# Second layer of a two-layer network: another order of one period's calls, other slots for four of them

## The chip, the cores and the metric

The kernel runs on one core of a Trainium2 chip. The core has five engines that work side by side, each through its own queue in order: PE (TensorE, matrix products), ACT (ScalarE, functions of single elements), DVE (VectorE) and POOL (GpSimd) for arithmetic on tiles, SP (SyncE), which here only starts transfers. They wait for one another through semaphores. The metric is the device time of one execution in microseconds, the median of several runs.

## The reference

Input is x, 8 images of 128 channels and 128 x 128 points, float32. The first layer (a dilated convolution, Fourier transforms, channel attention and a gate) takes about the first 2,000 us and is not changed. The second layer, on its result x:

```python
y = conv2d(x, conv_w, padding=1) + conv_b              # 3x3, 128 -> 128 channels
seq = y.reshape(B * H * W, 8, 16)                      # 8 tokens of 16 channels
xz = einsum('nld,ed->nle', seq, in_proj_w); xi, z = split(xz)
xc = silu(causal_depthwise_conv(xi) + conv1d_b)        # 32 channels, 4 taps
dt, Bm, Cm = split(xc @ x_proj_w.T, [1, 17])
dt = softplus(dt * dt_proj_w + dt_proj_b)
h = exp(dt * A) * h + dt * Bm * xc                     # 16 states per channel, over the 8 tokens
ym = (sum(h * Cm, states) + D * xc) * silu(z)
out = ym @ out_proj_w.T
xp = silu(group_norm(out.reshape(B, C, H, W), 4 groups))
return x + xp
```

## The kernel before

The second layer works in blocks of four image rows (512 points in the free dimension), 256 blocks in all. The partitions hold channels for the convolution, then channel and token for the projections, then 8 channels x 16 states for the recurrence, with one token and 16 channels (two such halves, 1,024 elements) as the unit of work. Such a unit is called by a number s from 0 to 15: token s // 2, half s % 2. What happens to one unit:

- `spread_a(i, s, slot)` and `spread_u(i, s, slot)` (L840, PE) multiply dt by A, or spread the input u, onto 128 partitions, into one of three PSUM tiles s0, s1, s2, the slots. Each uses two groups of 32 rows of PE's array: those of even s are the lower ones, those of odd s the upper ones.
- `exps(i, s)` (L851, ACT) takes the exponential in place in the slot.
- `inject(i, s)` (L864, DVE; L862, POOL for s = 4 and 5) makes the new tile h = spread u times B.
- `decay(i, s)` (L875, DVE) multiplies the exponential in its slot by h of unit s - 2; for s = 12 and 13 (L873) it writes a new h, for 14 and 15 (L870) it multiplies into a product with C.
- `add(i, s)` (L880, DVE), for s = 2 to 11, adds the slot to h, and the slot is free.
- `weigh(i, s)` (L886, POOL) makes hc = h times C, and `collect(i, t)` (L987, PE) sums the states of token t into PSUM tile yps. `cross` (L892, DVE), `end_products` (L935, POOL), `ends_sum` (L952 and L957, PE), `own_terms` (L964, DVE) and `own_add` (L971, PE) do the same for the last tokens without an h of their own.

Around these stand, per block, the nine taps of the convolution (`conv`, L734, PE), `biased` (L741, ACT, the bias, out of PSUM tile pm), `turn` (L747, PE, four transposes of that result into pm), `turned` (L752, ACT), the projections (`project_x`, `project_z`, `project_dt`, `project_bc`, `project_out`, PE) with the functions behind them (`silu_x`, `silu_z`, `softplus`, `states`, ACT), `inputs` (L792, POOL, u = dt times xc), `skip` (L980, ACT, D times xc into yps), `gated` (L994, DVE), `result` and `spread_of` (ACT, sums for the norm), and `last_load`, `last_act`, `last_sum`, `last_store`, which finish an image that has its norm. Once in 32 blocks `norm` runs the group norm's statistics through DVE, PE and ACT.

SP starts the transfers: `lay_states` copies rows of B and C (tiles all_b and all_c) over 128 partitions into bb0, bb1, cc0, cc1; `lay_first`, `lay_own`, `lay_own_first`, `lay_ends`, `lay_cross` and `store_inputs` with `lay_inputs` move the pieces for the last tokens and for POOL's injects.

The order is written out by hand. The tuple ORDER (from L1093) lists 154 calls as (function, ahead, arguments), and the loop behind it runs the whole tuple for i from -4 to 258, each call on block i + ahead. One pass is called a period. Five engines are set to keep that order (no scheduler moves anything), so the tuple gives each engine's queue, and a call that waits holds up all calls behind it on its engine. Semaphores follow from the tiles: a spread waits until its slot's last reader is done, a new h or hc until the readers of the tile nine allocations before are done (pools of 9), turn, the projections and `ends_sum` until tile pm is free.

Of the kernel before, what the change touches and what calls it, by code (L numbers as in the profile page):

```python
# [595 lines left out]
def layer1(ctx, tc, x1, w1, c1, out):  # L596
# [489 lines left out]
    def last_store(i):  # L1086
# [4 lines left out]

    FIRST = (lay_ends, lay_first, lay_own, lay_own_first, end_products, ends_sum, own_terms)
    ORDER = (  # L1093
        (load, 4), (store_inputs, 0, 2), (last_store, -2), (exps, -1, 10), (lay_first, -1), (end_products, -1),
        (exps, -1, 13), (lay_own, -1), (add, -1, 11), (conv, 2, 0, 0), (project_z, 1, 0), (silu_z, 1),
        (decay, -1, 10), (decay, -1, 13), (conv, 2, 1, 0), (add, -1, 10), (weigh, -1, 8), (spread_u, 0, 2, 2),
        (spread_a, -1, 15, 1), (gated, -1, 0), (inject, 0, 2), (spread_a, -1, 12, 0), (conv, 2, 2, 0),
        (exps, -1, 15), (lay_cross, -1), (weigh, -1, 15), (lay_inputs, 0, 2), (weigh, -1, 13), (weigh, -1, 10),
        (project_x, 1, 2, 0), (exps, -1, 12), (lay_states, 0, 1, 0), (silu_x, 1), (decay, -1, 15),
        (decay, -1, 12), (cross, -1, 15), (conv, 2, 3, 0), (spread_u, 0, 1, 0), (spread_a, 0, 2, 1),  # L1100
        (spread_u, 0, 7, 2), (exps, 0, 2), (inject, 0, 1), (conv, 2, 4, 0), (skip, -1, 1), (spread_u, 0, 3, 0),
        (inputs, 0, 1), (inject, 0, 7), (spread_a, -1, 14, 2), (exps, -1, 14), (conv, 2, 5, 0),
        (collect, -1, 4), (decay, 0, 2), (inject, 0, 3), (conv, 2, 6, 0), (weigh, -1, 14), (add, 0, 2),
        (spread_a, 0, 3, 0), (lay_states, 0, 0, 1), (spread_u, 0, 8, 1), (cross, -1, 14), (conv, 2, 7, 0),
        (last_act, -1), (lay_ends, 0), (weigh, -1, 11), (decay, -1, 14), (collect, -1, 5), (inject, 0, 8),
        (weigh, -1, 12), (exps, 0, 3), (decay, 0, 3), (conv, 2, 8, 0), (keep, -2), (spread_u, 0, 9, 1),
        (spread_a, 0, 4, 2), (lay_own_first, -1), (add, 0, 3), (biased, 2), (inject, 0, 4), (norm, -3),
        (turn, 2), (exps, 0, 4), (inject, 0, 9), (decay, 0, 4), (last_load, 0), (turned, 2),
        (spread_a, 0, 6, 0), (exps, 0, 6), (spread_of, -2), (ends_sum, -1), (weigh, 0, 2), (spread_a, 0, 5, 1),
        (add, 0, 4), (own_terms, -1), (exps, 0, 5), (inject, 0, 5), (decay, 0, 6), (spread_u, 0, 6, 2),  # L1110
        (project_dt, 1, 0, 0), (inject, 0, 6), (decay, 0, 5), (collect, -1, 7), (spread_a, 0, 7, 2),
        (collect, -1, 6), (softplus, 1, 0), (exps, 0, 7), (project_bc, 1, 0), (weigh, 0, 3), (own_add, -1, 1),
        (lay_states, 0, 1, 1), (inputs, 1, 0), (states, 1, 0), (add, 0, 6), (last_sum, -1), (weigh, 0, 4),
        (add, 0, 5), (decay, 0, 7), (gated, -1, 1), (spread_u, 0, 11, 1), (spread_a, 0, 8, 0), (skip, 0, 0),
        (add, 0, 7), (project_bc, 1, 1), (weigh, 0, 5), (exps, 0, 8), (inject, 0, 11), (collect, 0, 1),
        (decay, 0, 8), (spread_u, 0, 10, 2), (lay_states, 1, 0, 0), (states, 1, 1), (weigh, 0, 7),
        (spread_a, 0, 9, 1), (inject, 0, 10), (add, 0, 8), (project_dt, 1, 1, 0), (own_add, 0, 0),
        (exps, 0, 9), (decay, 0, 9), (collect, 0, 2), (spread_a, 0, 11, 0), (softplus, 1, 1), (add, 0, 9),
        (spread_u, 1, 0, 2), (project_out, -1, 0), (inject, 1, 0), (weigh, 0, 6), (project_out, -1, 1),
        (exps, 0, 11), (result, -1), (spread_a, 0, 10, 1), (decay, 0, 11), (spread_a, 0, 13, 2), (weigh, 0, 9),  # L1120
        (collect, 0, 3),
    )

    TR = 2 * RB
# [42 lines left out]
def network(tc, x, w0, w1, c0, c1, out):  # L1167
    B = x.shape[0]
    with tc.tile_pool(name="dram", bufs=1, space=DRAM) as dram:
        x1 = [dram.tile([C, H, W], F32, name=f"x1_{b}") for b in range(B)]  # L1170
        layer0(tc, x, w0, c0, x1)
        layer1(tc, x1, w1, c1, out)
# [73 lines left out]
```

## Time and profile before

| | |
|---|---|
| Median of 3 runs | 13,595.54 us (13,595.24 to 13,596.91) |
| Profiled execution, its span | 13,597.71 us, 13,594.9 us |
| PE busy | 13,227.2 us (97%) |
| DVE busy | 11,943.4 us (88%) |
| POOL busy | 11,940.1 us (88%) |
| ACT busy | 10,091.1 us (74%), of it table loads for exponentials 1,599.9 us |
| DMA queue of SP | 60.0% of 16 engines |

The first 2,000 us are the first layer; the second fills the rest, and drains in the last 200 us or so. PE's matrix instructions overlap and their ends are modelled, so PE's busy share overstates how full it is. A line of the timeline gives start, duration, engine, source line and operation, output and inputs, shapes, count, and in brackets the idle time before with what ended it. A line of the waits gives total us, times and the longest.

### The profile page before, as it was taken

How to read it: one execution, taken by the hardware profiler on the slowest of the kernel's cores; microseconds unless marked ns; L12 is line 12 of the kernel's file. 1: busy time of each engine (PE TensorE's matmuls, PEld its weight loads, DVE VectorE, ACT ScalarE, POOL GpSimd, SP SyncE). 2: the span in 40 equal slices, each digit the busy share in tenths (PEclk: the TensorE clock that was granted, in tenths of full speed). 3: DMA queues.
4: the chain of work that ended last, by engine and by line, in shares of the span. 5: the costliest groups of instructions: out<-in, count | busy, mean ns of one | idle time of the engine just before them, and what ended most of it. 6: DMA issues, size and time to landing. Idle time of an engine off the chain costs nothing. (4 is left out here: it accounts for less than half of the span.)

```text
span 13594.9 us, 255193 instructions
## 1 busy us (share of the span) xinstructions
PE 13227.2 (97%) x97850; PEld 4812.6 (35%) x97850; DVE 11943.4 (88%) x11710; ACT 10091.1 (74%) x11827; POOL 11940.1 (88%) x6533
## 2 busy tenths in 40 slices
PE   9999999999999999999999999999999999999996
PEld 5676663333333333332333333332333333323332
DVE  3343349999999999999999999999999999999997
ACT  3454367777788878887888878887888788878886
POOL 6766659999899999999999989999999999989996
PEclk9999999999999999999999999999999999999998
DMA  4544455555566666666666666666666666666666
GB/s 132 160 133 125 144 128 135 134 129 135 137 154 149 152 145 153 152 150 147 150 154 150 149 146 151 153 149 148 148 154 152 144 153 150 154 142 154 150 150 177
DMA packets 1183640, 1996.65 MB, mean 147 GB/s; under 512 B 149616, under 2 KB 411824, under 8 KB 1174224
## 3 DMA queue, kind: packets, MB, share of 16 engines
q1 hardware_dynamic: 1181840, 1977.82, 60.0%
q8 instruction: 769, 12.60, 0.4%
q14 instruction: 455, 3.73, 0.1%
q10 hardware_dynamic: 576, 2.50, 0.1%
HBM read 687.75 MB, written 218.10 MB: 67 GB/s over the span
## 5 line engine op out<-in xcount | busy, mean ns | idle before, releaser
L886 POOL TENSOR_TENSOR hc<-h,cc 128x1024 f32<-128x1024 f32 x3584 | 8424.7, 2375 | 308.2 <-PE s L840 219.9
L851 ACT ACTIVATE s<-s 128x1024 f32<-128x1024 f32 x3584 | 3558.2, 1005 | 1185.5 <-PE s L840 1166.7
L840 PE MATMUL s<-dt,m_a 32*128 32x512 f32 x14336 | 3525.2, 638 | 17.0 <-DVE h L880 14.5
L875 DVE TENSOR_TENSOR s<-s,h 128x1024 f32<-128x1024 f32 x2560 | 3134.3, 1224 | 46.0 <-ACT s L851 22.4
L864 DVE TENSOR_TENSOR h<-s,bb 128x1024 f32<-128x1024 f32 x2560 | 3100.6, 1215 | 55.2 <-DMA bb<-all_b 20.2
L880 DVE TENSOR_TENSOR h<-s,h 128x1024 f32<-128x1024 f32 x2560 | 3094.7, 1217 | 54.5 <-DVE s L875 1.8
L840 PE MATMUL s<-u,l_ct 32*128 32x512 f32 x10240 | 2892.2, 641 | 50.2 <-DVE h L873 18.4
L734 PE MATMUL pm<-xin,l_wt 128*32 128x508 f32 (+3 forms) x18432 | 2409.2, 595 | 6.2 <-DVE wk L650 5.5
L987 PE MATMUL yps<-hc,l_ct 128*32 128x512 f32 x14336 | 1889.6, 598 | 61.5 <-ACT yps L980 55.9
L851 ACT ACT_TABLE_LOAD x1247 | 1599.9, 1283 | 235.8 <-DVE h L880 136.6
L840 PEld LDWEIGHTS s<-dt,m_a 32*128 32x128 f32 x14336 | 969.1, 183 | 1275.0 <-DVE h L880 629.7
L840 PEld LDWEIGHTS s<-u,l_ct 32*128 32x128 f32 x10240 | 768.2, 183 | 1438.5 <-DVE h L880 521.2
L862 POOL TENSOR_TENSOR h<-ud,bb 128x1024 f32<-128x1024 f32 x512 | 1220.8, 2384 | 2.4 <-DMA ud<-uw 2.4
L792 POOL TENSOR_TENSOR u<-dt,xc 128x512 f32<-128x512 f32 x512 | 656.0, 1281 | 458.5 <-ACT dt L787 456.6
L734 PEld LDWEIGHTS pm<-xin,l_wt 128*32 128x32 f32 x18432 | 469.3, 109 | 1588.4 <-issue 1586.7
L987 PEld LDWEIGHTS yps<-hc,l_ct 128*32 128x32 f32 x14336 | 394.9, 109 | 1288.8 <-issue 1024.3
L870 DVE TENSOR_TENSOR hc<-s,hc 128x1024 f32<-128x1024 f32 x512 | 623.6, 1218 | 199.4 <-ACT s L851 191.0
L787 ACT ACT_TABLE_LOAD x511 | 655.6, 1283 | 40.9 <-PE pm L782 23.9
L980 ACT ACTIVATE yps<-xc,l_wt 128x512 f32<-128x512 f32 x511 | 352.1, 689 | 403.3 <-DVE ym L994 403.3
L873 DVE TENSOR_TENSOR h<-s,h 128x1024 f32<-128x1024 f32 x512 | 621.5, 1214 | 0.0
L892 DVE TENSOR_TENSOR hc<-s,cbx 128x1024 f32<-128x1024 f32 x512 | 620.4, 1212 | 0.0
L782 PE MATMUL pm<-xc,m_dt 128*32 128x512 f32 x4096 | 545.6, 605 | 1.4 <-ACT yT L752 0.7
(202 smaller groups left out, 15362.6 us busy)
## 6 DMA issues: line engine op xcount, KB each, us to landing
cc<-all_c SPq DMA_DIRECT2D x1792, 256.0 KB, 5.5
bb<-all_b SPq DMA_DIRECT2D x1536, 256.0 KB, 5.7
ud<-uw SPq DMA_DIRECT2D x1024, 256.0 KB, 4.1
xin<-x SPq DMA_DIRECT2D x152, 768.0 KB, 5.1
xin<-x SPq DMA_DIRECT2D x112, 640.0 KB, 6.6
us<-u SPq DMA_DIRECT2D x1025, 64.0 KB, 1.9
cbx<-cb SPq DMA_DIRECT2D x512, 128.0 KB, 2.4
gn<-xr SPq DMA_DIRECT2D x256, 256.0 KB, 2.2
```

The source lines that it names most:

```text
L734: nc.tensor.matmul(d["pm"][c, a:b, wa:wb], convw[:, t, c], xin[:, r + dy + a - lo:r + dy + b - lo, wa + dx:wb + dx], start=(k == 0), stop= ...
L787: nc.scalar.activation(d["dt", hf], flat(d["pm"]), AF.Softplus, bias=wf("dt_b"))
L792: nc.gpsimd.tensor_mul(d["u", hf], d["dt", hf], d["xc"][:, hf, :])
L840: nc.tensor.matmul(d[name, s][:, q], m[a:a + DI, t % LP, :], d[src, t // LP][a:a + DI, :], start=True, stop=True)
L851: nc.scalar.activation(da, da, AF.Exp)
L862: nc.gpsimd.tensor_mul(h, d["ud", t][:, k:k + GP, :], state_row(i, "bb", t))
L864: nc.vector.tensor_mul(h, d["ups", s], state_row(i, "bb", t))
L870: nc.vector.tensor_mul(d["hc", s], da, d["hc", s])
L875: nc.vector.tensor_mul(da, da, d["h", s - GP])
L880: nc.vector.tensor_add(h, d["da", s], h)
L886: nc.gpsimd.tensor_mul(hc, d["h", s if t < L - 1 else s - GP], state_row(i, "cc", t))
L987: nc.tensor.matmul(d["yps"][g * DI:(g + 1) * DI], gather[:, t % LP, :], d["hc", GP * t + g // GP][:, g % GP], start=False, stop=t in LAST, ...
```

## The change

ORDER holds the same 154 calls in another order. The first and last call of the tuple are others: what stood in the last third or so of a pass now stands at the front of the next, with its block number lowered by one, so that the same work is done. Apart from that turn of the cycle, many calls stand elsewhere among their neighbours, on all engines. Four spreads have other slots: `spread_u` 6 and `spread_a` 4 go to slot 1, `spread_u` 9 and `spread_a` 5 to slot 2. No call is added or removed, and nothing outside the tuple changes.

```diff
@@ -1091,34 +1091,34 @@

     FIRST = (lay_ends, lay_first, lay_own, lay_own_first, end_products, ends_sum, own_terms)
     ORDER = (
-        (load, 4), (store_inputs, 0, 2), (last_store, -2), (exps, -1, 10), (lay_first, -1), (end_products, -1),
-        (exps, -1, 13), (lay_own, -1), (add, -1, 11), (conv, 2, 0, 0), (project_z, 1, 0), (silu_z, 1),
-        (decay, -1, 10), (decay, -1, 13), (conv, 2, 1, 0), (add, -1, 10), (weigh, -1, 8), (spread_u, 0, 2, 2),
-        (spread_a, -1, 15, 1), (gated, -1, 0), (inject, 0, 2), (spread_a, -1, 12, 0), (conv, 2, 2, 0),
-        (exps, -1, 15), (lay_cross, -1), (weigh, -1, 15), (lay_inputs, 0, 2), (weigh, -1, 13), (weigh, -1, 10),
-        (project_x, 1, 2, 0), (exps, -1, 12), (lay_states, 0, 1, 0), (silu_x, 1), (decay, -1, 15),
-        (decay, -1, 12), (cross, -1, 15), (conv, 2, 3, 0), (spread_u, 0, 1, 0), (spread_a, 0, 2, 1),
-        (spread_u, 0, 7, 2), (exps, 0, 2), (inject, 0, 1), (conv, 2, 4, 0), (skip, -1, 1), (spread_u, 0, 3, 0),
-        (inputs, 0, 1), (inject, 0, 7), (spread_a, -1, 14, 2), (exps, -1, 14), (conv, 2, 5, 0),
-        (collect, -1, 4), (decay, 0, 2), (inject, 0, 3), (conv, 2, 6, 0), (weigh, -1, 14), (add, 0, 2),
-        (spread_a, 0, 3, 0), (lay_states, 0, 0, 1), (spread_u, 0, 8, 1), (cross, -1, 14), (conv, 2, 7, 0),
-        (last_act, -1), (lay_ends, 0), (weigh, -1, 11), (decay, -1, 14), (collect, -1, 5), (inject, 0, 8),
-        (weigh, -1, 12), (exps, 0, 3), (decay, 0, 3), (conv, 2, 8, 0), (keep, -2), (spread_u, 0, 9, 1),
-        (spread_a, 0, 4, 2), (lay_own_first, -1), (add, 0, 3), (biased, 2), (inject, 0, 4), (norm, -3),
-        (turn, 2), (exps, 0, 4), (inject, 0, 9), (decay, 0, 4), (last_load, 0), (turned, 2),
-        (spread_a, 0, 6, 0), (exps, 0, 6), (spread_of, -2), (ends_sum, -1), (weigh, 0, 2), (spread_a, 0, 5, 1),
-        (add, 0, 4), (own_terms, -1), (exps, 0, 5), (inject, 0, 5), (decay, 0, 6), (spread_u, 0, 6, 2),
-        (project_dt, 1, 0, 0), (inject, 0, 6), (decay, 0, 5), (collect, -1, 7), (spread_a, 0, 7, 2),
-        (collect, -1, 6), (softplus, 1, 0), (exps, 0, 7), (project_bc, 1, 0), (weigh, 0, 3), (own_add, -1, 1),
-        (lay_states, 0, 1, 1), (inputs, 1, 0), (states, 1, 0), (add, 0, 6), (last_sum, -1), (weigh, 0, 4),
-        (add, 0, 5), (decay, 0, 7), (gated, -1, 1), (spread_u, 0, 11, 1), (spread_a, 0, 8, 0), (skip, 0, 0),
-        (add, 0, 7), (project_bc, 1, 1), (weigh, 0, 5), (exps, 0, 8), (inject, 0, 11), (collect, 0, 1),
-        (decay, 0, 8), (spread_u, 0, 10, 2), (lay_states, 1, 0, 0), (states, 1, 1), (weigh, 0, 7),
-        (spread_a, 0, 9, 1), (inject, 0, 10), (add, 0, 8), (project_dt, 1, 1, 0), (own_add, 0, 0),
-        (exps, 0, 9), (decay, 0, 9), (collect, 0, 2), (spread_a, 0, 11, 0), (softplus, 1, 1), (add, 0, 9),
-        (spread_u, 1, 0, 2), (project_out, -1, 0), (inject, 1, 0), (weigh, 0, 6), (project_out, -1, 1),
-        (exps, 0, 11), (result, -1), (spread_a, 0, 10, 1), (decay, 0, 11), (spread_a, 0, 13, 2), (weigh, 0, 9),
-        (collect, 0, 3),
+        (load, 4), (add, -1, 7), (lay_states, -1, 1, 1), (gated, -2, 1), (decay, -1, 8), (states, 0, 1),
+        (lay_states, 0, 0, 0), (project_dt, 0, 1, 0), (skip, -1, 0), (lay_first, -1), (lay_own, -1),
+        (spread_u, -1, 10, 2), (inject, -1, 10), (spread_a, -1, 9, 1), (exps, -1, 9), (store_inputs, 0, 2),
+        (add, -1, 8), (decay, -1, 9), (collect, -1, 1), (weigh, -1, 6), (own_add, -1, 0), (collect, -1, 2),
+        (spread_u, 0, 0, 2), (weigh, -1, 7), (softplus, 0, 1), (spread_a, -1, 11, 0), (end_products, -1),
+        (lay_cross, -1), (project_out, -2, 0), (add, -1, 9), (inject, 0, 0), (project_out, -2, 1),
+        (spread_a, -1, 10, 1), (spread_a, -1, 13, 2), (lay_states, 0, 1, 0), (exps, -1, 11), (result, -2),
+        (decay, -1, 11), (exps, -1, 10), (conv, 2, 0, 0), (add, -1, 11), (exps, -1, 13), (decay, -1, 10),
+        (decay, -1, 13), (collect, -1, 3), (add, -1, 10), (project_z, 1, 0), (conv, 2, 1, 0),
+        (spread_u, 0, 2, 2), (weigh, -1, 8), (last_sum, -2), (silu_z, 1), (spread_a, -1, 15, 1),
+        (spread_a, -1, 12, 0), (gated, -1, 0), (weigh, -1, 9), (conv, 2, 2, 0), (inject, 0, 2),
+        (weigh, -1, 15), (project_x, 1, 2, 0), (exps, -1, 15), (exps, -1, 12), (cross, -1, 15),
+        (conv, 2, 3, 0), (decay, -1, 12), (spread_u, 0, 1, 0), (decay, -1, 15), (inject, 0, 1), (silu_x, 1),
+        (weigh, -1, 11), (spread_a, 0, 2, 1), (spread_u, 0, 7, 2), (conv, 2, 4, 0), (exps, 0, 2),
+        (inject, 0, 7), (spread_u, 0, 3, 0), (skip, -1, 1), (spread_a, -1, 14, 2), (lay_states, 0, 0, 1),
+        (weigh, -1, 10), (conv, 2, 5, 0), (decay, 0, 2), (weigh, -1, 14), (lay_own_first, -1), (exps, -1, 14),
+        (inject, 0, 3), (inputs, 0, 1), (add, 0, 2), (conv, 2, 6, 0), (last_act, -1), (conv, 2, 7, 0),
+        (spread_u, 0, 6, 1), (lay_inputs, 0, 2), (spread_a, 0, 3, 0), (weigh, -1, 13), (conv, 2, 8, 0),
+        (decay, -1, 14), (collect, -1, 4), (cross, -1, 14), (exps, 0, 3), (inject, 0, 6), (inject, 0, 4),
+        (decay, 0, 3), (last_store, -2), (biased, 2), (norm, -3), (turn, 2), (weigh, -1, 12),
+        (spread_a, 0, 4, 1), (spread_u, 0, 9, 2), (spread_of, -2), (turned, 2), (add, 0, 3), (inject, 0, 9),
+        (ends_sum, -1), (spread_a, 0, 5, 2), (spread_a, 0, 6, 0), (exps, 0, 4), (last_load, 0), (decay, 0, 4),
+        (own_terms, -1), (inject, 0, 5), (weigh, 0, 2), (exps, 0, 5), (project_dt, 1, 0, 0), (exps, 0, 6),
+        (collect, -1, 7), (add, 0, 4), (own_add, -1, 1), (spread_u, 0, 8, 1), (decay, 0, 5), (softplus, 1, 0),
+        (lay_ends, 0), (weigh, 0, 3), (add, 0, 5), (decay, 0, 6), (spread_a, 0, 7, 2), (project_bc, 1, 0),
+        (inject, 0, 8), (collect, -1, 5), (add, 0, 6), (inputs, 1, 0), (exps, 0, 7), (decay, 0, 7),
+        (weigh, 0, 4), (spread_u, 0, 11, 1), (states, 1, 0), (spread_a, 0, 8, 0), (weigh, 0, 5),
+        (project_bc, 1, 1), (keep, -2), (inject, 0, 11), (exps, 0, 8), (collect, -1, 6),
     )

     TR = 2 * RB
```

## The prediction

> **What bounds the kernel now.** Read first: the busy table by stretches, for a stretch in the middle of the second layer.
>
> ```profile
> core 0: us, PE busy (x) PEld busy (x) DVE busy (x) ACT busy (x) POOL busy (x), PEclk, DMA share, GB/s
> 6000.00:7000.00 1000.00, 983.28 (x7466) 306.18 (x7460) 969.31 (x881) 805.36 (x890) 927.95 (x444) 0.99 0.63 150
> ```
>
> PE, DVE and POOL are all above 92%, so busy shares don't name the bound. Read next: the timeline of DVE. One period (one block of four image rows) takes 44.49 us: the median over 105 periods without a group norm, each 44.5. With the entry, the drain and the first layer around them: 256 x 44.49 = 11,389 us, seven periods with a norm add 12.9 us each (a pair with a norm takes 101.9, 2 x 44.49 = 89.0), and 2,115 us lie outside; together the span, 13,594.9. The profiled execution was 13,597.71 us, the median of the timed runs 13,595.54, so I apply the difference to the median.
>
> ```profile
> 6033.17 1.21 DVE L880 TENSOR_TENSOR h<-s,h 128x1024 f32<-128x1024 f32 x1
> 6034.30 0.68 DVE L994 TENSOR_TENSOR ym<-yps,zs 128x512 f32<-128x512 f32 x1
> 6034.90 1.21 DVE L864 TENSOR_TENSOR h<-s,bb 128x1024 f32<-128x1024 f32 x1
> 6036.86 1.23 DVE L870 TENSOR_TENSOR hc<-s,hc 128x1024 f32<-128x1024 f32 x1 [0.75 <-ACT s L851]
> ...
> 6053.17 1.22 DVE L875 TENSOR_TENSOR s<-s,h 128x1024 f32<-128x1024 f32 x1
> 6054.49 1.23 DVE L880 TENSOR_TENSOR h<-s,h 128x1024 f32<-128x1024 f32 x1
> 6055.64 0.68 DVE L964 TENSOR_TENSOR own<-pm,us 128x512 f32<-128x512 f32 x1
> 6056.23 1.22 DVE L875 TENSOR_TENSOR s<-s,h 128x1024 f32<-128x1024 f32 x1
> 6057.36 1.21 DVE L864 TENSOR_TENSOR h<-s,bb 128x1024 f32<-128x1024 f32 x1
> ```
>
> Starts of independent neighbours are 1.13 apart (6056.23 to 6057.36), a short one (own, gated) takes 0.60. A decay (L875) followed at once by the add (L880) that needs it takes 1.32 (6053.17 to 6054.49): a dependent neighbour costs 0.13, and 0.20 if it also waits for another engine. A period has 36 long and 3 short DVE instructions: 36 x 1.133 + 3 x 0.60 = 42.6. The missing 1.9 us can be listed: five dependent neighbours (adds 3, 9, 11 at 0.13 to 0.14, add 4 and decay 7 at 0.20 and 0.19: 0.79), the wait shown at 6036.86 (0.83 over the plain step), inject 1 (0.18), inject 7 and decay 3 (0.06 each): 1.92. So DVE's own chain accounts for the whole period: **DVE with the waits in its path is the bound**.
>
> The table of DVE's waits over 5,000 us has the one large entry:
>
> ```profile
> DVE hc L870 <- ACT s L851: 81.0, 107, 1.0
> ```
>
> ACT and PE show where it and the next tight place come from:
>
> ```profile
> 6034.46 1.28 ACT L851 ACT_TABLE_LOAD   x1 [0.53 <-DVE h L880]
> 6035.76 1.93 ACT L851 ACTIVATE s<-s 128x1024 f32<-128x1024 f32 x2
> ...
> 6048.59 1.01 ACT L851 ACTIVATE s<-s 128x1024 f32<-128x1024 f32 x1
> 6050.59 0.69 ACT L741 ACTIVATE y<-pm,l_wt 128x512 f32<-128x512 f32 x1 [0.99 <-PE pm L734]
> ```
>
> ```profile
> 6049.48 1.03 PE L734 MATMUL pm<-xin,l_wt 128*32 128x508 f32 x8
> 6050.45 0.70 PE L840 MATMUL s<-u,l_ct 32*128 32x512 f32 x2
> 6050.46 0.70 PE L840 MATMUL s<-dt,m_a 32*128 32x512 f32 x2
> 6051.52 0.66 PE L747 MATMUL pm<-l_ct,y 128*128 128x128 f32 x4
> 6052.18 1.13 PE L840 MATMUL s<-dt,m_a 32*128 32x512 f32 x4
> 6053.25 1.07 PE L952 MATMUL pm<-hc,l_ct 128*32 128x512 f32 x8
> ```
>
> Add 10 ends at 6034.38 and frees slot 1; the exponential's table load waits for it, and 2.48 us later decay 15 starts: a slot's way round PE and ACT. On PE, two spreads on different row groups together take 1.07 (6050.45 to 6051.52), as one alone does (6052.18 to 6053.25); conv, turn and ends_sum groups take 0.86, 0.66 and 1.86, and going to a spread adds 0.1.
>
> **The change part by part.** The loop is the same cycle of 154 calls. The starting point is turned back by some ten microseconds, and calls at the new front have their block number lowered by one. The counts per period stay on each engine (DVE 39, ACT 27 and 10 table loads, POOL 20, SP 35 transfers), so only waits can change. All times below are from the start of add 11 in a period.
>
> *From inject 0 to inject 7* DVE keeps its order but for one swap: decay 15, decay 12, cross 15 becomes cross 15, decay 12, decay 15. PE and ACT keep theirs but for collect 3 behind the first conv. Decay 15 waits for ACT and POOL and starts 0.10 after its exponential; the cross waits for ACT last, as decay 3 does, which starts 0.03 after. I take -0.06; bounds 0 and -0.07. The 0.83 wait itself stays. POOL's product for decay 15 ends at 5.9, needed at 9.4: covered by 3.5 us, at 1 us per us beyond that.
>
> *From inject 7 to the next inject 0* DVE has another order. Dependent neighbours: adds 3 (0.14), 5 (0.20, it waits for POOL too) and 9 (0.13), beside add 11: 0.60 against 0.79, **-0.19**. Here the Trainium skill, "VectorE: DVE Perf Modes", section "The DRAIN you can't avoid", speaks against a gain: it says that chained DVE operations cost the same with and without semaphores, so nothing would come of moving dependent instructions apart. The row says 1.26 to 1.33 against 1.13. By the rule the 0.19 falls out and the sum below ends at +0.10 a period, 13,624 us; I take the row.
>
> *PE* loses a group: spreads of slots 6 and 7 stood alone, now all are in pairs (11 groups, not 12), 1.07 + 0.1 us. Since DVE is the bound I cost that at nothing; the cover is DVE's 44.4 us against about 43 of PE's groups. But conv 7, conv 8 now stand earlier and turn comes straight after collect 4. Biased (L741) can't run before exponential 3 ends (19.77 with the -0.06): it runs 19.69 to 20.38. Turn starts at 20.43 (0.05 is what spreads take after DVE), with PE idle from 19.7, the pair (4, 9) at 21.09, its end 22.23. Inject 9 waits for DMA, PE and POOL, so 0.11 more: 22.34, against 22.21 in DVE's own order: **+0.13**; bounds +0.06 (start 0.04 after PE) and +0.25 (turn 0.14 behind ACT, as collect 1 starts behind skip). Queued behind turn on PE: the pair, ends_sum, the pair (5, 6), project_dt. Decay 4 needs exponential 4 by 23.47, it ends at 23.3; own 24.60, ends_sum ends 24.1; decay 5 at 26.33, exponential 5 ends 26.2. All just in time, 0 to +0.05.
>
> *spread_a 7* stands in a pair with spread_u 8 but needs slot 2 from add 5 (28.9), so it runs 0.95 behind and the pair is none; inject 8 (29.9) and 11 (33.3) still find theirs done (29.2, 33.1). spread_a 8 waits for add 6 (32.3); then project_bc, collect 6, project_dt follow, and spread_u 10 ends at 37.24, inject 10 starts at 37.35 instead of 37.33: **+0.03**, bounds 0 and +0.1.
>
> *POOL*: weigh 12 waits for collect 4 (19.9), 1.1 us idle; weigh 15 for decay 13, 1.1; weigh 3 for collect 7, 0.4. POOL's own work is 41.7, so 2.8 a period is free, and the waits replace others (before: 1.1 for softplus and 0.85 for add 9 in the period shown). Inject 0 needs weigh 7 (40.3) at 42.0. Cost nothing; beyond 1.7 us of lateness it is 1 to 1.
>
> *SP*: lay_first with its two transfers now stands behind the eight of lay_states and ahead of store_inputs. The tile all_b is ready at 32.0 (32.5 before), so bb0 is issued from 32 to 37, as in the period before (32.6 to 37.6), for inject 0 at 42. Lay_first lands near 41, and end_products waits under 1 us on POOL, within its slack. The cbx transfers land by 45, used at 51.4. Keep, last_store, last_load, lay_ends and lay_inputs move to the end of the queue with over 5 us each. Nothing.
>
> *Group norm* (seven times): ACT and PE idle as before, but inject 9 behind it now needs the pair (4, 9) from a PE that runs its first groups at half speed (turn took 1.12 there, a spread 2.08), where before that pair was done. DVE's blocked tensor_scalar (6.2 us, until POOL pauses) gets its pause about 0.7 earlier, since weigh 3 now waits for an add behind the norm. About +0.4 each, +3 us.
>
> Sum: -0.06 - 0.19 + 0.13 + 0.03 = -0.09 a period, x 256 = -23, +3: **-20 us, 13,576**.
>
> **The rivals.** *PE is the bound after all.* For it: 983 of 1000 busy. Against: the list above fills the period, and a modelled end makes PE look full. The lost group of 1.17 less the 0.7 idle at turn is 0.5 a period: -128, 13,468.
> *The turn chain costs more* (the one on the other side): the place is biased, turn, pair (4, 9), inject 9. Each 0.1 us by which turn starts later than 20.43 is 26 us; from 0.08 the gain is gone, from 0.19 it is slower by 0.2%. For it: PE idles there, behind an ACT that has just been held by a table load. Against: a DVE release reaches a spread in 0.05. At 0.3: +57, about 13,650.
> *Dependent neighbours cost nothing extra* (the rule): for it, only the skill's measurement of copies; against it, five steps of 1.26 to 1.33 in every period. 13,624.
>
> **How the numbers follow.** A measurement of this kernel tells 0.2%, 27 us, from no change. Forecast 0.57, its own range 13,550 to 13,600; with a middle of -20 some four in ten of that lie below -27: faster 0.22, same 0.35. PE-bound 0.09, faster. Turn chain, with waits like it that I don't see, 0.26: slower 0.24, same 0.02. The rule 0.08: half and half. Together faster 0.31, same 0.41, slower 0.28. The range 13,535 to 13,650 leaves out the PE-bound case and the far end of the turn chain.
>
> **What would show it.** In the changed trace: period 44.40; DVE's large wait at L892 in place of L870, 0.75 us; a wait of L864 on PE near 0.1 us once a period, ten long steps behind it; turn with PE idle about 0.7 before it; dependent steps of 1.26 to 1.33 four times. Wrong if DVE shows new waits of 0.2 us or more a period (PE or POOL), if turn starts more than 0.15 behind biased, or if POOL's idle exceeds 3 us a period.

## The result, and the profile after

The changed kernel takes 13,551.8 us (median of 7 runs, 13,549.5 to 13,555.5) where the kernel before, run beside it, takes 13,595.2 us: a ratio of 0.9967, 95% interval 0.9957 to 0.9977. That is 43 us or 0.33% faster. The forecast was -20 us, 13,576.

The profiled execution has a span of 13,553.0 us, 41.9 less than before. Its busy table for the same stretch as before (columns as shown above):

```profile
6000.00:7000.00 1000.00, 972.02 (x7490) 304.29 (x7482) 974.31 (x885) 803.69 (x893) 928.34 (x444) 0.99 0.67 150
```

PE's share fell from 983 to 972 in spite of the shorter period (the lost group), DVE's rose from 969 to 974. The timeline of DVE in one plain period of the changed kernel, the same places as shown of before:

```profile
6018.75 1.21 DVE L864 TENSOR_TENSOR h<-s,bb 128x1024 f32<-128x1024 f32 x1
6020.64 1.23 DVE L892 TENSOR_TENSOR hc<-s,cbx 128x1024 f32<-128x1024 f32 x1 [0.68 <-ACT s L851]
...
6032.22 1.21 DVE L864 TENSOR_TENSOR h<-s,bb 128x1024 f32<-128x1024 f32 x1
6033.41 1.23 DVE L875 TENSOR_TENSOR s<-s,h 128x1024 f32<-128x1024 f32 x1
6034.68 1.23 DVE L880 TENSOR_TENSOR h<-s,h 128x1024 f32<-128x1024 f32 x1
6035.90 1.23 DVE L864 TENSOR_TENSOR h<-s,bb 128x1024 f32<-128x1024 f32 x1
```

Inject 2 to cross 15 (L864 to L892) steps 1.89, where decay 15 stepped 1.96 in the kernel before. Add 3, directly behind the decay 3 it needs, steps 1.27. The step to inject 9 (6034.68 to 6035.90) is 1.22, 0.09 over a plain one; that is the new wait that the prediction placed here. Between inject 6 and decay 3 lie 1.19, 0.06 over a plain step, as there was at decay 3 before. Over 107 such periods the median is 44.42 us, where 44.40 was forecast and 44.49 was before.

DVE's waits over 5,000 us have the large entry at the new place, and no other of its size:

```profile
DVE hc L892 <- ACT s L851: 76.2, 112, 0.7
```

Then ACT and PE where the other wait comes from, exponential 3 with what stands ahead of it, and turn:

```profile
6030.24 0.81 ACT L1077 ACTIVATE v<-v,bi,sc 128x512 f32<-128x512 f32 x1
6031.07 1.28 ACT L851 ACT_TABLE_LOAD   x1
6032.37 1.01 ACT L851 ACTIVATE s<-s 128x1024 f32<-128x1024 f32 x1
6033.29 0.68 ACT L741 ACTIVATE y<-pm,l_wt 128x512 f32<-128x512 f32 x1
...
6034.02 0.66 PE L747 MATMUL pm<-l_ct,y 128*128 128x128 f32 x4 [0.58 <-ACT y L741]
```

PE idles 0.58 before turn, as foreseen. But look one line up: exponential 3 starts right behind the table load that follows last_act (L1077). ACT had no idle time ahead of it. This becomes important below, at e_act.

**Where 42 us went.** All periods of each trace, by the starts of turn (L747), give a sum. The gain of a row is worked out from its medians or means; the last two rows are sums over the single periods:

| stretch | before | after | together |
|---|---|---|---|
| plain periods from the second image on, about 224 | 44.49 | 44.42 | -15 |
| periods of the first image, about 32 | 44.69 | 44.25 | -14 |
| two periods with a norm in them, 7 times (mean) | 101.80 | 100.61 | -7, beyond what the plain periods give |
| single periods of the later images off the median | | | -4 |
| entry (to the third period) and drain | | | -2 |

A plain period gives 0.07 where 0.09 was forecast. A third of the gain comes from the first image, where the forecast's 0.09 a period would have made 3 us, and a sixth from the norms, for which it had +3. In the last two rows no cause was followed up: single periods differ from the median by up to 1.1 us in the kernel before, and of the kernels below that leave entry and drain as they were, some show a drain 3 us shorter too, and some don't.

### The profile page after: what moved, and what is told of

It is laid out like the page before. It is cut to its first block, busy times and chain, and to the rows that moved or that the text cites. A ratio compares the mean times of both kernels' runs of the same rounds, so it can differ in the third digit from the quotient of the medians.

```text
span 13553.0 us, 255075 instructions
## 1 busy us (share of the span) xinstructions
PE 13065.8 (96%) x97850; PEld 4778.4 (35%) x97850; DVE 11962.2 (88%) x11710; ACT 10061.7 (74%) x11827; POOL 11935.9 (88%) x6533
## 5 line engine op out<-in xcount | busy, mean ns | idle before, releaser
L840 PE MATMUL s<-dt,m_a 32*128 32x512 f32 x14336 | 3302.7, 638 | 11.7 <-DVE h L880 8.1
L864 DVE TENSOR_TENSOR h<-s,bb 128x1024 f32<-128x1024 f32 x2560 | 3110.9, 1219 | 69.2 <-DMA bb<-all_b 19.5
L875 DVE TENSOR_TENSOR s<-s,h 128x1024 f32<-128x1024 f32 x2560 | 3132.9, 1224 | 4.4 <-ACT s L851 4.3
L734 PE MATMUL pm<-xin,l_wt 128*32 128x508 f32 (+3 forms) x18432 | 2323.8, 597 | 5.9 <-DVE wk L650 5.2
L840 PEld LDWEIGHTS s<-dt,m_a 32*128 32x128 f32 x14336 | 940.3, 183 | 794.0 <-issue 222.9
L987 PEld LDWEIGHTS yps<-hc,l_ct 128*32 128x32 f32 x14336 | 439.3, 110 | 1115.7 <-issue 1097.6
L892 DVE TENSOR_TENSOR hc<-s,cbx 128x1024 f32<-128x1024 f32 x512 | 624.5, 1220 | 175.8 <-ACT s L851 175.8
L935 POOL TENSOR_TENSOR cb<-bcs 128x256 f32<-128x256 f32 x257 | 187.0, 728 | 454.2 <-DMA bcs<-all_c 196.3
```

The lines of the kernel that those rows point to most:

```text
L734: nc.tensor.matmul(d["pm"][c, a:b, wa:wb], convw[:, t, c], xin[:, r + dy + a - lo:r + dy + b - lo, wa + dx:wb + dx], start=(k == 0), stop= ...
L840: nc.tensor.matmul(d[name, s][:, q], m[a:a + DI, t % LP, :], d[src, t // LP][a:a + DI, :], start=True, stop=True)
L864: nc.vector.tensor_mul(h, d["ups", s], state_row(i, "bb", t))
L875: nc.vector.tensor_mul(da, da, d["h", s - GP])
L892: nc.vector.tensor_mul(cr, d["da", s], d["cbx"].broadcast_to([P, GP, N]))
L987: nc.tensor.matmul(d["yps"][g * DI:(g + 1) * DI], gather[:, t % LP, :], d["hc", GP * t + g // GP][:, g % GP], start=False, stop=t in LAST, ...
```

## The experiments

Times are medians; the kernel before was run beside each (13,594 to 13,598). "From the changed kernel" is against its 13,552; as runs of one kernel spread over 2 to 16 us, differences of a few us there are not safe, and the periods say more. The periods are medians from each trace:

| kernel | first image | later images | us |
|---|---|---|---|
| before | 44.69 | 44.49 | 13,595 |
| changed | 44.25 | 44.42 | 13,552 |
| e_dep | 44.39 | 44.42 | 13,560 |
| e_apart | 44.69 | 44.86 | 13,663 |
| e_turn | 44.49 | 44.49 | 13,581 |
| e_both | 44.93 | 44.93 | 13,693 |
| e_split | 45.46 | 45.46 | 13,824 |
| b_cross | 44.62 | 44.42 | 13,573 |
| b_norm | 44.69 | 44.49 | 13,584 |
| b_seen | 44.42 | 44.49 | 13,582 |
| e_act | 44.25 | 44.25 | 13,512 |
| e_act_dep | 44.39 | 44.39 | 13,549 |
| e_best | 44.24 | 44.61 | 13,589 |

**Does a dependent neighbour cost time?** (e_dep)

```diff
-        (inject, 0, 3), (inputs, 0, 1), (add, 0, 2), (conv, 2, 6, 0), ...
+        (inputs, 0, 1), (add, 0, 2), (inject, 0, 3), (conv, 2, 6, 0), ...
```

> The changed kernel with one pair of DVE steps exchanged: add 2 now stands directly behind the decay 2 that it needs, inject 3 behind it; nothing else is moved. Theory (a dependent neighbour costs 0.13 us on DVE, and DVE's chain is the bound): add 2's step becomes 1.26 us, the period 44.42 + 0.13 = 44.55, 256 x 0.13 = +33 us against the changed kernel's 13,552, so 13,585, 10 us under the kernel before. Inject 3 ends 1.26 later, at 16.55 after add 11, and spread_a 3 needs its slot at 16.9, so nothing else is late. Rival, the Trainium skill, VectorE: DVE Perf Modes, section The DRAIN you can't avoid (chained DVE operations cost the same whether or not they wait for each other): 13,552, step 1.13. If PE were the bound: 13,552 as well, the longer step hidden.

Measured: 13,559.8 us (ratio to before 0.9972, 0.9961 to 0.9982), +8 from the changed kernel; neither the 33 nor nothing. The timeline of DVE in a later image, decay 2, add 2, inject 3, and further on inject 6, decay 3:

```profile
6029.11 1.22 DVE L875 TENSOR_TENSOR s<-s,h 128x1024 f32<-128x1024 f32 x1
6030.36 1.23 DVE L880 TENSOR_TENSOR h<-s,h 128x1024 f32<-128x1024 f32 x1
...
6034.90 1.22 DVE L864 TENSOR_TENSOR h<-s,bb 128x1024 f32<-128x1024 f32 x1
6036.03 1.22 DVE L875 TENSOR_TENSOR s<-s,h 128x1024 f32<-128x1024 f32 x1
```

The new dependent step is 1.25 (1.26 in the median), so the cost is there. But the step to decay 3 is now 1.13 instead of 1.19, and the one to inject 9 is 1.16 instead of 1.22: the two small waits behind it give the 0.13 back, and inject 9 starts at 22.29 after add 11 in both kernels. So from there on something else than DVE sets the time. In the first image, where no last_act is run, the same edit costs 44.39 - 44.25 = 0.14 in every period. Theory and rival both fall as stated: the cost of 0.13 is real, and whether it lies on the path depends on the stretch.

**Which chain is it?** The first image has no last_load, last_act, last_sum and last_store, and of these last_act stands just ahead of exponential 3. In e_act it stands ahead of silu_z, which then needs no table load of its own; the other three stay:

```diff
-        ... (last_sum, -2), (silu_z, 1), (spread_a, -1, 15, 1),
+        ... (last_sum, -2), (last_act, -1), (silu_z, 1), (spread_a, -1, 15, 1),
...
-        ... (conv, 2, 6, 0), (last_act, -1), (conv, 2, 7, 0),
+        ... (conv, 2, 6, 0), (conv, 2, 7, 0),
```

> The changed kernel with last_act put directly ahead of silu_z on ACT, which has the same function table, so that exponential 3 no longer stands behind last_act and its two table loads. Theory (from decay 12 to inject 9 the chain of PE's groups, exponential 14, last_act, exponential 3, biased, turn and the pair (4, 9) sets the time, and DVE has 0.13 us of room beside it): decay 3 and inject 9 no longer wait (0.06 and 0.09), silu_z is 0.7 later and the table load behind it, which waits for add 10, 0 to 0.04: the period falls to the 44.25 that the changed kernel shows in its first image, where last_act is missing, or 44.29 at most: 220 x -0.13 to -0.17 = -29 to -37 us against the changed kernel's 13,552: 13,515 to 13,523. Rival (PE's groups alone set that stretch, whatever ACT does): 13,552.

Measured: 13,512.3 us (ratio to before 0.9938, 0.9926 to 0.9950), -40 from the changed kernel, and a period of 44.25 in all images. That is 3 us less than the theory's range. The timelines of ACT (last_act, silu_z with no load between them), of PE (collect 4, turn) and of DVE (inject 6, decay 3) in this kernel:

```profile
6002.94 0.81 ACT L1077 ACTIVATE v<-v,bi,sc 128x512 f32<-128x512 f32 x1
6003.66 1.00 ACT L776 ACTIVATE zs<-s 128x1024 f32<-128x1024 f32 x1
```

```profile
6018.84 1.04 PE L987 MATMUL yps<-hc,l_ct 128*32 128x512 f32 x8
6019.84 0.66 PE L747 MATMUL pm<-l_ct,y 128*128 128x128 f32 x4
```

```profile
6018.66 1.22 DVE L864 TENSOR_TENSOR h<-s,bb 128x1024 f32<-128x1024 f32 x1
6019.79 1.22 DVE L875 TENSOR_TENSOR s<-s,h 128x1024 f32<-128x1024 f32 x1
```

Turn follows collect 4 without idle time, and decay 3 no longer waits. Exponential 3 is 0.69 earlier (18.07 after add 11, where it was 18.76). Silu_z is 0.6 later and delays nothing: the exponential behind it starts at 5.99 in both. This version beats both kernels, 0.62% under the kernel before. The edit does two things at once: it takes last_act out of the way of exponential 3, and ACT runs 8 table loads a period for 10. Moving last_act to a place where it shares no load was not tried.

With the chain out of the way, the dependent neighbour was tried once more (e_act_dep: both edits together).

> The kernel with last_act ahead of silu_z, and in addition add 2 directly behind the decay 2 that it needs, as in the run with the two exchanged. Theory (a dependent neighbour costs 0.13 us, and nothing takes it up now that decay 3 and inject 9 do not wait): 256 x 0.13 = +33 us against the kernel with last_act moved alone: 13,548 to 13,556. Rival (the cost is never on the path[...]): no difference between these two.

Measured: 13,548.9 us, +37 from e_act (+29 by the two spans), and 44.39 for 44.25 in every period. So here the 0.13 is paid in full in each period. The Trainium skill ("VectorE: DVE Perf Modes", section "The DRAIN you can't avoid") measured copies, with and without semaphores, and does not say whether they depended on each other; carried over to this dependent addition of 128x1024, its "costs nothing extra" would give 0, and 0.13 was measured.

**Can a dependence simply be moved apart?** (e_apart)

```diff
-        (lay_cross, -1), (project_out, -2, 0), (add, -1, 9), (inject, 0, 0), (project_out, -2, 1),
+        (lay_cross, -1), (project_out, -2, 0), (inject, 0, 0), (add, -1, 9), (project_out, -2, 1),
```

> The changed kernel with inject 0 put between decay 9 and add 9, so that one dependent neighbour fewer is left in the period (three in place of four). Theory: add 9 steps 1.13 in place of 1.26, the period 44.29, 256 x -0.13 = -33 us against the changed kernel: 13,519. Add 9 ends 1.0 us later, and the pair of spreads for slots 10 and 13, that waited for inject 0 anyway, then runs together: exponential 10 is 0.25 later and ends 0.1 before decay 10 needs it. If that margin is not there, decay 10 waits 0.1 and the gain is nothing. Rival (dependence costs nothing, the page's rule): 13,552. If PE were the bound: 13,552.

Measured: 13,663.4 us, +112 from the changed kernel: a miss by 144. The steps, in the changed kernel and here: add 9 and inject 0 have 1.26 + 1.14, now inject 0 and add 9 have 1.50 + 1.14; decay 11 has 1.13, now 1.32. Inject 0 needs spread_u 0, which ends at 41.03; moved to 40.76 it waits until 41.13. And decay 11 multiplies by the state of slot 9, which is add 9's output: the dependent pair was not dissolved, it only moved one place on, and costs 0.19 there. DVE's waits name no engine for the first:

```profile
DVE h L864 <- issue: 33.7, 113, 1.2
```

**What does turn's place cost?** (e_turn; e_both has this and the edit of e_apart)

```diff
-        (decay, 0, 3), (last_store, -2), (biased, 2), (norm, -3), (turn, 2), (weigh, -1, 12),
-        (spread_a, 0, 4, 1), (spread_u, 0, 9, 2), (spread_of, -2), ...
+        (decay, 0, 3), (last_store, -2), (biased, 2), (norm, -3), (weigh, -1, 12),
+        (spread_a, 0, 4, 1), (spread_u, 0, 9, 2), (turn, 2), (spread_of, -2), ...
```

> The changed kernel with turn put behind the pair of spreads (4, 9) on PE, so that the pair fills the 0.7 us in which PE waits for biased. Theory (inject 9 waits 0.09 us because the pair comes behind turn): inject 9 steps 1.13 in place of 1.22, and the later turn costs 0 to 0.04 at own and at decay 5, whose exponential then ends just in time: -0.05 to -0.09 a period, -13 to -23 us against the changed kernel: 13,529 to 13,539. Rival (the wait only moves on to decay 5 or own): 13,552. If PE were the bound, the 0.7 us of filled idle time a period would give -180 us: 13,372.

> The changed kernel with both edits: inject 0 between decay 9 and add 9, and turn behind the pair (4, 9). Theory: the two gains lie at different places of DVE's chain and add up, -0.18 to -0.22 a period: -46 to -56 us, 13,496 to 13,506. Rival (dependence costs nothing): 13,529 to 13,539 from turn alone.

Measured: 13,581.0 and 13,692.9 us, +29 and +141 from the changed kernel. In e_turn inject 9 steps 1.14, so its wait did come from the turn ahead of the pair. But turned (L752) is 0.44 later, ends_sum waits for it and runs 0.2 later, the pair (5, 6) behind ends_sum too; exponential 5 ends at 26.32 instead of 26.11, and decay 5 steps 1.28 instead of 1.13. Together +0.07 a period (0.24 in the first image), and +1.2 for each norm. The wait moved on, and grew, further than the rival said. Nor was PE's idle time filled; it moved behind turn, ahead of ends_sum:

```profile
6044.46 1.07 PE L952 MATMUL pm<-hc,l_ct 128*32 128x512 f32 x8 [0.68 <-ACT yT L752]
```

So this run says nothing for or against PE as the bound. The two edits add up (112 + 29 = 141): they lie in different stretches.

**Is there room on PE?** (e_split: the pair of spreads for slots 6 and 3 is taken apart)

```diff
-        ... (last_act, -1), (conv, 2, 7, 0),
-        (spread_u, 0, 6, 1), (lay_inputs, 0, 2), (spread_a, 0, 3, 0), ...
+        ... (last_act, -1),
+        (spread_u, 0, 6, 1), (conv, 2, 7, 0), (lay_inputs, 0, 2), (spread_a, 0, 3, 0), ...
```

> The changed kernel with conv 7 put between the spreads of slots 6 and 3 on PE, so that these two no longer run as a pair: PE has 1.07 + 0.1 us more in each period, as it had in the kernel before. Theory (DVE is the bound, PE takes it up in the 0.6 us idle before turn and in those behind it): spread 3 is 0.2 later, turn at the latest 0.1, so 0 to +0.1 a period: 13,552 to 13,578. Rival (PE is the bound): +1.1 x 256 = +280 us, 13,830.

Measured: 13,823.9 us, +272: what the rival said, not the theory. The timeline of PE at spread_u 6, and DVE's waits over 5,000 us:

```profile
6036.37 1.13 PE L840 MATMUL s<-u,l_ct 32*128 32x512 f32 x4 [0.43 <-DVE h L880]
```

```profile
DVE s L875 <- ACT s L851: 101.6, 113, 0.9
```

Spread_u 6 needs slot 1 from add 2, and conv 7 had covered that; without it PE waits 0.43. The second spread alone takes 1.06 more, and two more changes between conv and spread 0.2. Spread 3 and collect 4 end 1.68 later. Exponential 3, which last_act's loads had held up by 0.7 anyway, starts 0.94 later, and 1.04 arrives at decay 3 (0.95) and inject 9 (0.10): the period is 45.46. So PE has less room than the forecast's period sum let it seem: in a plain period of the changed kernel its timeline has only 0.9 us of idle time (0.05, 0.58 and 0.23). In the changed kernel its groups follow each other without a gap from decay 12's end (9.4) to collect 4 (19.8). Up to spread 14 (14.2) they lie on the chain to inject 9, which goes on over ACT: exponential 14, table load, last_act, table load, exponential 3. The groups behind spread 14 have 0.6 to 0.7 us of room beside that, and this edit asks for 1.68.

**The parts of the change, one at a time, on the kernel before.** First the order of cross 15 (b_cross):

```diff
-        ... (silu_x, 1), (decay, -1, 15),
-        (decay, -1, 12), (cross, -1, 15), (conv, 2, 3, 0), ...
+        ... (silu_x, 1),
+        (cross, -1, 15), (decay, -1, 12), (decay, -1, 15), (conv, 2, 3, 0), ...
```

> The kernel before with one part of the change alone: cross 15, decay 12, decay 15 on DVE in place of decay 15, decay 12, cross 15. Theory (the cross starts 0.03 behind the exponential, the decay, which waits for POOL too, 0.10): the wait step is 1.90 in place of 1.96, -0.06 x 256 = -15 us: 13,580. Rival (a step behind a wait costs the same whatever it waits for): 13,595.

Measured: 13,572.9 us, -21 (ratio 0.9983, 0.9975 to 0.9991). The step is 1.90 for 1.96, the period 44.42 for 44.49: -0.07 x 256 = -17, the rest lies in entry, drain and norms. The theory holds.

Then the norm's place (b_norm):

```diff
-        ... (lay_own_first, -1), (add, 0, 3), (biased, 2), (inject, 0, 4), (norm, -3),
+        ... (lay_own_first, -1), (biased, 2), (inject, 0, 4), (norm, -3), (add, 0, 3),
```

> The kernel before with add 3 put behind the seven group norms on DVE, as it stands in the changed kernel; periods without a norm keep their instructions and order. Theory (the norm's tensor_scalar on DVE waits until POOL pauses, and weigh 3, which needs add 3, then has to wait and gives the pause early): a pair of periods with a norm takes 100.5 to 100.8 us in place of 101.9, 7 x -1.3 = -9 us: 13,586. Rival (the pause comes from weigh 12, which waits for collect 4 in the changed kernel alone): a pair keeps 101.9, and the kernel 13,595.

Measured: 13,584.2 us, -10 (ratio 0.9993, 0.9985 to 1.0001, so the times alone don't tell it from no change); in the traces the two periods with a norm have a mean of 100.3 for 101.8 (1.2 less, with the period behind them), and the plain ones stay at 44.49. The norm's third instruction on DVE, in the kernel before:

```profile
7845.49 6.16 DVE L1038 TENSOR_SCALAR dm<-st,mv 128x32 f32<-128x32 f32 x1
```

in b_norm, with the POOL instruction that stands next:

```profile
7842.28 5.13 DVE L1038 TENSOR_SCALAR dm<-st,mv 128x32 f32<-128x32 f32 x1
...
7852.75 2.35 POOL L886 TENSOR_TENSOR hc<-h,cc 128x1024 f32<-128x1024 f32 x1 [5.38 <-DVE h L880]
```

and in the changed kernel, with its two followers:

```profile
7823.34 0.95 DVE L1038 TENSOR_SCALAR dm<-st,mv 128x32 f32<-128x32 f32 x1
7824.33 2.27 DVE L1039 TENSOR_TENSOR dm<-dm 128x32 f32<-128x32 f32 x1
7826.64 2.27 DVE L1040 SCALAR_TENSOR_TENSOR dm<-dm,st 128x32 f32<-128x32 f32 x1
```

An instruction of 32 columns takes 6.16 us: it ends at 7851.65, when the last of POOL's three products in a row is done (7849.29 + 2.33). In b_norm POOL has to stop at weigh 3, which needs add 3 from behind the norm (5.38 idle), and the blocked instruction takes 1.0 less. In the changed kernel each of the three ends where a POOL instruction does, though the next POOL instruction follows at once: 5.5 together for 6.5.

The seven norms of one kernel are not alike: before, the third instruction takes 0.9 to 1.6 in the first three and 6.2 to 6.4 in the others. Over all seven, the three blocked instructions take 6.3 in the kernel before, 5.1 in b_norm and 5.5 in the changed kernel, and DVE's waits behind the norm sum to 2.3, 2.3 and 2.1. So the gain lies mainly in the blocked instructions, and the place of add 3 alone brings at least as much as the whole change. The weigh 12 rival falls. Which of POOL's instructions a blocked one has to sit out stays open.

Then the first image (b_seen):

```diff
         nc.scalar.copy(d["yT"], flat(d["pm"]))
+        if 2 <= i < 36:
+            seen = wk2.tile([P, 1], F32, name="seen")
+            nc.scalar.copy(seen, st8[i - 2]["u", 1][:, 0:1])
```

> The kernel before with one more small ACT instruction (a copy of 128 x 1, about 0.2 us) in the first 34 blocks, behind turned; it reads u, so that ACT has waited for POOL by the time softplus comes. Then softplus' activation itself carries the wait for PE, and its table load none, as it is from the second image on. Theory (the table load that waits for PE makes softplus 0.6 later in the first image, exponential 7 late, and decay 7 wait 0.4): the first image's period falls from 44.69 to 44.3 or less, 30 x -0.4 = -12 us: 13,583. Rival (the first image's long period has another cause, such as the transfers that are missing there): 13,595.

Measured: 13,582.4 us, -12 (ratio 0.9992, 0.9985 to 0.9998). The first image's period falls from 44.69 to 44.42, 32 x -0.27 = -9, and the drain gave 3. Softplus' table load in the kernel before, and DVE's waits in that stretch:

```profile
2511.83 1.28 ACT L787 ACT_TABLE_LOAD   x1 [0.64 <-PE pm L782]
```

```profile
DVE s L875 <- ACT s L851: 8.6, 23, 0.4
```

and the same load in b_seen (its lines are three further down):

```profile
2507.73 1.28 ACT L790 ACT_TABLE_LOAD   x1
```

The 0.64 of idle time ahead of the load is gone, and with it the 23 waits of decay 7 (L875). Adding an instruction made the kernel faster. The reading that fits: softplus must see PE and POOL done; where ACT has already waited for POOL, the wait for PE stands at the activation, and the load runs early; where it hasn't, as in the first image, the load holds the wait for PE. The traces show where the wait for PE stands; that the wait for POOL pushes it to the load is argued, from the copy's effect alone. The expected 44.3 was too low: the rest of the way to the changed kernel's first image is cross 15 (-0.07), the dependent neighbours (-0.19) and inject 10 (+0.09): 44.42 - 0.17 = 44.25, as measured.

**One more place** (e_best: e_act and the second project_dt behind the spreads)

```diff
-        (lay_states, 0, 0, 0), (project_dt, 0, 1, 0), (skip, -1, 0), ...
-        (spread_u, -1, 10, 2), (inject, -1, 10), (spread_a, -1, 9, 1), (exps, -1, 9), ...
+        (lay_states, 0, 0, 0), (skip, -1, 0), ...
+        (spread_u, -1, 10, 2), (inject, -1, 10), (spread_a, -1, 9, 1), (project_dt, 0, 1, 0), (exps, -1, 9), ...
```

> The kernel with last_act ahead of silu_z, and in addition the second project_dt on PE put behind spread_u 10 and spread_a 9. Theory (inject 10 waits 0.09 us because spread_u 10 comes behind project_dt): inject 10 steps 1.13 in place of 1.22, softplus, which needs project_dt, starts 1.3 us after its new end, so 256 x -0.09 = -23 us against last_act moved alone: 13,492 to 13,500. Rival (the wait moves on to exponential 11 or own_add): as last_act moved alone.

Measured: 13,588.7 us, +76 from e_act. Inject 10 steps 1.13, as expected. But spread_u 10 still can't start before add 7 frees its slot (35.92), so PE idles 0.4 where project_dt had been. Collect 1, own_add, collect 2 and the pair (10, 13) run 0.5 later against DVE, exponentials 10 and 13 with them, then last_act, silu_z and the next table load; cross 15 steps 2.27 instead of 1.90. The gain expected did not come; the wait moved on, as the rival had it, but cost 76 us where the rival had none. In the first image, without last_act in that queue, the period is 44.24.

## Why the prediction was right, and where it was off

The sum for a plain period came out by the mechanisms named (-0.07 for -0.09). The result is twice the forecast all the same, and lies 2 us above the lower end of the forecast's own range, 13,550 to 13,600: some 27 of the 42 us come from places where the sum had next to nothing or the wrong sign. That they fell on the fast side, and no further, is luck.

**The step that was missed: "256 x 44.49".** The periods were taken to be all alike. The first image's took 44.69 in the kernel before, since decay 7 waited there for an exponential behind a late softplus. In the changed kernel decay 7 steps 1.13. The first image gives -14 us of the -42; the sum had -3 for it, and the late softplus alone is worth -9 (b_seen). The median over later periods could not show it; the first 30 periods had to be read apart.

**"About +0.4 each, +3 us" for the norms.** The sign was wrong: -1.05 each, -7. The prediction saw that POOL's pause comes earlier, and set it at 0.7, but charged the slow PE groups behind the norm at more. Inject 9 does wait there, 1.19 at each of the seven norms; but decay 4 no longer waits its 0.44, own waits 0.7 in place of 1.5, and the three blocked instructions are 0.8 shorter (means).

**Cross 15, -0.06:** measured -0.06 to -0.07, alone and in the change. Right.

**Dependent neighbours, -0.19:** the four steps are 1.26, 1.26, 1.27 and 1.33, as forecast, and the period holds the gain. The choice of the row over the rule was right: 0.13 on the path in e_act_dep and in the first image of e_dep. The new order from inject 7 on was not tried alone on the kernel before; its share is read from the steps. What the prediction did not see is that from decay 12 to inject 9 DVE has up to 0.13 of room, so a dependence there is free as long as last_act stands where it does.

**Inject 9, +0.13:** the mechanism is the one named (biased, turn, the pair, with PE idle before turn), its size 0.09. **Inject 10, +0.03:** 0.09, as spread_u 10 waits for add 7 and project_dt. Together 0.18 for 0.16. On POOL, end_products waits 1.5 in the median period where under 1 was expected, with no wait of note on DVE behind it.

**"The lost group costs nothing ... DVE with the waits in its path is the bound."** Only half right. PE's busy time fell by 161 us and the kernel's by 43, and the rival "PE is the bound after all" (13,468) failed: in e_act_dep 0.13 more on DVE, with PE's work unchanged, lengthens the period by 0.14. But the argument for DVE did not hold: steps taken from start to start, waits included, fill a period on any engine, so the list could not name the bound. And "at nothing" failed: e_split gives the group back, with 0.6 us of waits and changes beside it, and costs 272 us. The list of DVE's steps hid a second chain as tight as the first: PE's groups up to spread 14, exponential 14, last_act, exponential 3, biased, turn, the pair. The 0.06 at decay 3 was read as a fixed cost, and was the mark of this chain. On that stretch 1.68 us more of PE cost 1.04. Whether the lost group alone would gain anything in the kernel before was not tried.

**The turn chain costs more** (13,650) did not come true; its place was right, and e_turn shows how little is needed for its sign.

## What to carry to other kernels

A list of one engine's steps, waits included, always fills the period; look for waits of a few hundredths in it. Each can mark a second chain with no more room than that, as the 0.06 at decay 3 did, and an edit is paid or not by the stretch in which it lies. Read the first and last iterations apart from the middle: a missing instruction there can shift which instruction holds a wait. Look at what stands ahead of an exponential on the chain; here moving one activation away from it, next to one that shares its function table, was worth about as much as the whole change.

## What was not expected of the hardware

- A table load on ACT can hold the wait for the matmul that its activation needs: 0.64 us of idle time ahead of the load, and a 0.20 us copy that reads POOL's result beforehand removes it.
- An instruction of 32 columns on DVE took from 0.9 to 6.4 us in one kernel, the shown ones ending where an instruction of POOL did.
- A DVE step that needs the result of the one before it takes 1.26 for 1.13, and 1.33 where it waits for POOL too.
